# A decoder block's attention on one core: output projections in whole groups of four, spread over the last two batches, and one token tile of the last batch projected before the next stage

## The chip, the cores and the metric

The kernel runs on one core of one Trainium2 chip. The metric is the device time of a run in microseconds (us). The kernel before took 2040.6 us as the median of three runs (2039.63 to 2043.01). The profile is one further execution with the hardware profiler on.

## The reference

One pre-norm decoder block on x of 4 batches x 512 tokens x 512 features, all in fp32.

```python
x = x + attn(layernorm(x), weight_qkv, weight_proj)      # causal, 16 query heads, 4 key/value groups, D = 128
x = x + xattn(layernorm(x), ctx, ctx)                    # 32 query heads, 8 key/value heads, D = 16
x = x + ffn(layernorm(x), gate_w, w1, w2, w3, sw1, sw2, sw3)  # 8 experts, top 2, plus a shared expert

def attn(x, weight_qkv, weight_proj):
    qkv = einsum('bsh,ph->bsp', x, weight_qkv)           # per group: 4 query heads, a key, a value
    scores = where(causal, q @ k.T / sqrt(128), lowest)
    out = softmax(scores) @ v                            # 2048 features per token
    return einsum('bse,he->bsh', out, weight_proj)
```

Only the first line's attention and its neighbour, the cross-attention, are touched by the change.

## The kernel before

The program has three stages: causal attention (to about 889 us of the span), cross-attention with the shared expert as filler (to about 1600 us), and the routed experts.

**The attention stage** goes through 64 slots, one for each unit (b, g, h): batch, key/value group, query head of the group. I number them 0 to 63 in that order, so batch b has slots 16b to 16b + 15, and slot 4g + 3 of a batch ends a group. TensorE's instructions keep the program's order (`pinned_mm`, `Ordered`, L128 to 147), so the loop at L398 writes PE's order out by hand. The other engines' order is set by a scheduler, unless `pinned` is on. A slot does two things at once:

- `scores(u)` (L322) for its own unit: four score blocks of 128, 256, 384 and 512 columns (PE, tile `sc`); a causal mask and a negated maximum for each (DVE, `nmx`); an exp with its sum (ACT, `pr`); at the end the division by the sum (DVE).
- `attend(held)` (L359) for the unit before: the weights are transposed in four parts of 1, 2, 3 and 4 blocks (PE, `tp`), copied out of PSUM (`prT`: DVE, the second part ACT), multiplied with the values (`po`), and copied by ACT into `oT`.

Between these steps the loop drops single matmuls, called jobs, from two lists. `ahead` holds what the next slot needs: its query projection (`project`, L289: four jobs, tile `pq`, evicted by ACT into `qT`) and, ahead of a new group, the key projection as well (four more, `kT`). `waiting` holds what may come later: value projections (`values`, L267, tile `pv`) and, once a group of four heads is done, its output projections (`output`, L308): for each of four token tiles a product of four jobs (tile `pj`), which DVE then adds to x. A slot takes as many waiting jobs as `take` says: 8, 8, 0, 0 in the first group, then 4, 5, 5, 2 over a group's four slots. `room` tells how many jobs follow each of the eight steps; `ahead` is served first.

Every such product fills one PSUM tile with tag "mm", of which there are two (`product`, L253; the pool at L187 gives two to each of the tags `t`, `mm`, `sc`, `po`). So a product that is half done keeps one of the two until its last job. In a batch's last slot the next batch's normalised x is turned (`turn`, L243: four transposes, tile `xt`, copied by ACT into `xnT`), and the first projections of that batch follow at once. After a batch's first slot its sixteen value projections come in one piece. `norm_first` (L226) normalises batch 0 tile by tile: statistics and the scaling on DVE, the power -0.5 on GpSimd (POOL); it isn't pinned.

The last batch's output projections are left to the next stage. There, `fill` (L870) gets four products of sixteen jobs each (tile `pl`, one for each token tile, over all 16 heads), in one PSUM bank with tag "fill".

**The cross-attention stage** (L900) runs 32 units of 8 steps, numbered i. Step i computes two heads' scores row-wise for their maxima (`row_maxima`, PE `s`, DVE `cnmx`) and, 11 steps later (`LAG`), the same scores turned for the exponentials (`weights`, PE `s`, ACT `w`). Each of the two has three PSUM banks. Every second step, `gather` multiplies the weights with the values (`cpo`). Jobs of `fill` go first, around the transposes `tc` and `tx` (8 + 5 + 4 jobs, L894 to 899); then one per step for 11 steps; then, up to step 80 (`SWAP`), the rest is spread over every second step (L924):

```python
elif i < SWAP:
    if mstep % 2 == 0:
        run(fill, -(-2 * len(fill) // (SWAP - i)))
```

Of the kernel before, what the change touches and what calls it, by code (L numbers as in the profile page):

```python
# [8 lines left out]
F32 = mybir.dt.float32  # L9
BF16 = mybir.dt.bfloat16  # L10
AF = mybir.ActivationFunctionType
ALU = mybir.AluOpType
# [3 lines left out]
P = 128  # L16
B, S, HID = 4, 512, 512
NT = S // P
NC = HID // P
NKV, QPG, D = 4, 4, 128  # L20
# [10 lines left out]
EPS = 1e-5  # L31
# [4 lines left out]
def decoder_kernel(  # L36
# [15 lines left out]
    nc = tc.nc  # L52
# [80 lines left out]
    pinned_mm, pinned = True, False  # L133

    class Ordered:
# [12 lines left out]
    tensor, vector, scalar, gpsimd, sync = (  # L148
        Ordered(e) for e in (nc.tensor, nc.vector, nc.scalar, nc.gpsimd, nc.sync)
    )  # L150

    xb = [xpool.tile([P, NT, HID], F32, tag=f"x{b}", name=f"x{b}") for b in range(B)]
# [31 lines left out]
    with ExitStack() as ph:  # L184
        wp = ph.enter_context(tc.tile_pool(name="wattn", bufs=1))
        p2 = ph.enter_context(tc.tile_pool(name="a2", bufs=2))
# [6 lines left out]
        wqk, wpr = [], []  # L193
        for g in range(NKV):
            t = wp.tile([P, NC, (QPG + 1) * D], F32, tag=f"wqk{g}", name=f"wqk{g}")
# [5 lines left out]
            t = pj.tile([P, QPG, HID], F32, tag=f"wpr{g}", name=f"wpr{g}")  # L201
# [12 lines left out]
        xns, xnTs, vs, kTs, qTs, outs = {}, {}, {}, {}, {}, {}  # L214
# [10 lines left out]

        def norm_first():  # L226

            xns[0] = []
            for s in range(NT):
                xn = p2.tile([P, HID], F32, tag="xn", name=f"xn0_{s}", bufs=4)  # L230
                st = small.tile([P, 6], F32, tag="st", name=f"fst{s}")
                mv = small.tile([P, 2], F32, tag="fmv", name=f"fmv{s}")
                nc.vector.bn_stats(st, xb[0][:, s, :])
                nc.vector.bn_aggr(mv, st)
                rstd = small.tile([P, 1], F32, tag="frstd", name=f"frstd{s}")
                nc.vector.tensor_scalar(rstd, mv[:, 1:2], EPS, None, ALU.add)
                nc.gpsimd.tensor_tensor(rstd, rstd, mhalf[:, 0:1], ALU.pow)
                nc.vector.tensor_scalar(
                    xn, xb[0][:, s, :], mv[:, 0:1], rstd, ALU.subtract, ALU.mult
                )  # L240
                xns[0].append(xn)

        def turn(b, s):  # L243

# [8 lines left out]
        def product(name, operands, done):  # L253
            held = []

            def job(k, lhsT, rhs):
                if k == 0:
                    held.append(ps.tile([P, S], F32, tag="mm", name=name))
                tensor.matmul(
                    held[0], lhsT=lhsT, rhs=rhs, start=k == 0, stop=k == len(operands) - 1  # L260
                )
                if k == len(operands) - 1:
                    done(held[0])

            return [lambda k=k, o=o: job(k, *o) for k, o in enumerate(operands)]

        def values(b):  # L267
            jobs, vs[b] = [], {}
# [53 lines left out]
        def scores(u):  # L322

            b, g, h = u
            qT, kT = qTs.pop(u), kTs[b, g]
            pr = p2.tile([P, 10 * P], F32, tag="pr", name=f"pr{b}_{g}_{h}")
            nmx = small.tile([P, NT], F32, tag="nmx", name=f"nmx{b}_{g}_{h}")
            sm = small.tile([P, NT], F32, tag="sm", name=f"sm{b}_{g}_{h}")

            def part(i):  # L330
                n = (i + 1) * P
                sc = ps.tile([P, S], F32, tag="sc", name=f"sc{b}_{g}_{h}_{i}")
                tensor.matmul(
                    sc[:, :n], lhsT=qT[:, i * P : n], rhs=kT[:, :n], start=True, stop=True
                )
                nc.vector.tensor_tensor(  # L336
                    sc[:, i * P : n], sc[:, i * P : n], maskf, ALU.add
                )
                nc.vector.tensor_reduce(  # L339
                    nmx[:, i : i + 1], sc[:, :n], AX.X, ALU.max, negate=True  # L340
                )
                nc.scalar.activation(  # L342
                    pr[:, OFF[i] : OFF[i] + n],
                    sc[:, :n],
                    AF.Exp,
                    bias=nmx[:, i : i + 1],
                    accum_out=sm[:, i : i + 1],
                )

            def divide():  # L350
                rs = small.tile([P, NT], F32, tag="rs", name=f"rs{b}_{g}_{h}")
                nc.vector.reciprocal(rs, sm)
                for j in range(NT):
                    w = pr[:, OFF[j] : OFF[j] + (j + 1) * P]
                    nc.vector.tensor_scalar(w, w, rs[:, j : j + 1], None, ALU.mult)

            return pr, [lambda i=i: part(i) for i in range(NT)], divide
# [31 lines left out]


        units = [(b, g, h) for b in range(B) for g in range(NKV) for h in range(QPG)]
        norm_first()
        for s in range(NT):
            turn(0, s)
        for job in project(0, 0, QPG) + project(0, 0, 0):
            job()
        waiting, ahead, held = values(0), [], None
        for u in units + [None]:  # L398
            between, turns = [lambda: None] * NT, []
            take = 4  # L400
            if u is not None:
                b, g, h = u
                pr, between, divide = scores(u)
                if (b, g) == (0, 0):
                    take = 8 if h < 2 else 0
                else:
                    take = (4, 5, 5, 2)[h]
                if (g, h) == (NKV - 1, 1) and b + 1 < B:
                    norm(b + 1)
                if h + 1 < QPG:  # L410
                    ahead = project(b, g, h + 1)
                elif g + 1 < NKV:
                    ahead = project(b, g + 1, QPG) + project(b, g + 1, 0)
                elif b + 1 < B:
                    turns = [lambda s=s: turn(b + 1, s) for s in range(NT)]

            room = [1, 1, 1, 1, 1, 1, 0, 2] if held else [1, 1, 1, 1, 0, 0, 0, 0]
            total = min(take, len(waiting)) + len(ahead) + (8 if turns else 0)
            for k in (1, 2, 0, 3, 7, 5, 4) * 2:
                room[k] += sum(room) < total  # L420
            for k in (5, 4, 0, 3, 2, 1) * 2:
                room[k] -= sum(room) > total and room[k] > 0
            steps = attend(*held) if held else []
            for k in range(2 * NT):
                if k < NT:
                    between[k]()
                    if turns:
                        turns.pop(0)()
                        if not turns:
                            ahead = project(b + 1, 0, QPG) + project(b + 1, 0, 0)  # L430
                elif steps:
                    steps.pop(0)()
                for _ in range(room[k]):
                    some = ahead or waiting
                    if some:
                        some.pop(0)()
            for job in ahead:
                job()
            ahead = []
            for step in steps:  # L440
                step()
            if u is not None:
                divide()
            if held:
                b_, g_, h_ = held[0]
                if h_ == QPG - 1 and b_ < B - 1:
                    waiting += output(b_, g_)
                if h_ == QPG - 1 and g_ == NKV - 1 and b_ < B - 1:
                    for job in values(b_ + 1):
                        job()  # L450
            held = (u, pr) if u is not None else None
        assert not waiting
        last_outs = [outs[B - 1, g] for g in range(NKV)]


# [114 lines left out]
    with ExitStack() as ph:  # L570
        p1 = ph.enter_context(tc.tile_pool(name="c1", bufs=1))
        p2 = ph.enter_context(tc.tile_pool(name="c2", bufs=2))
# [29 lines left out]
        for b in range(B):  # L602
            t = p1.tile([P, NT, XKV * XD], F32, tag=f"ctx{b}", name=f"ctx{b}")
# [264 lines left out]
            return ps.tile([P, S], F32, tag=tag, name=name, bufs=3 if tag == "s2" else 1)  # L868

        jobs, fill, po, last, oT = [], [], None, None, None  # L870
        for s in range(NT):
            group(
                fill,
                bank,
                f"pl{s}",
                [
                    (last_outs[g][h][:, s * P : (s + 1) * P], wpr[g][:, h, :])
                    for g in range(NKV)
                    for h in range(QPG)
                ],  # L880
                add_to(B - 1, s),
            )
# [8 lines left out]
        moments, turn = enter(0)  # L891
        run(moments, len(moments))
        pinned = True
# [6 lines left out]
        for i in range(NU * 8 + LAG + 4):  # L900
            n, step = divmod(i, 8)
# [34 lines left out]
            b, u = divmod(n, XKV)  # L936
            if b < B - 1:
                if u == XKV - 3 and step == 0:
                    moments, turn = enter(b + 1)
# [12 lines left out]
            if oT is not None and mstep == 3:  # L952
                add_heads(*oT)
                if oT[0] % XKV == XKV - 1 and oT[0] < NU - 1:
                    b = oT[0] // XKV
                    parts, tokens = route(b)
# [15 lines left out]
        parts, tokens = route(B - 1)  # L972
# [3 lines left out]
        parts = logits(B - 1, single, lambda lg: chosen.extend(choose(B - 1, lg)))  # L976
# [343 lines left out]
```

## Time and profile before

| what | value |
|---|---|
| median of three runs | 2040.6 us |
| the profiled execution | 2043.63 us |
| its span, first to last instruction | 2041.7 us |
| mean granted TensorE clock | 0.996 |
| first matmul | 8.89 us |
| first score of slot 0 | 20.78 us |
| first `pl` job | 889.42 us |
| first score of the cross-attention | 907.53 us |
| last `pl` job | 1082.96 us |

In the rows that follow, PE is TensorE's matmuls, PEld its weight loads, DVE VectorE, ACT ScalarE, POOL GpSimd and SP the queue that issues most DMAs. Almost all matmuls have line 141, that of the helper which keeps their order, so they are told apart by tile names, out<-in. An fp32 matmul has two records, a transpose one. A row of the timeline has its start, the time that it covers, engine, line, operation, tiles, shapes, the number of instructions merged into it, and, in brackets, idle time ahead of it with the engine that ended it. A row of the waits has who waited for whom, the total in us, how often, and the longest.

### The profile page before, as it was taken

Reading aid. Unit: us, or ns where it says so; the run is one execution under the profiler, and the core shown is the slowest. Engines: PE = TensorE matmul, PEld = TensorE weight load, DVE = VectorE, ACT = ScalarE, POOL = GpSimd, SP = SyncE. Lnnn points to the kernel's source line nnn. Section 1 sums busy time; section 2 is a strip of 40 time slices with the busy share of each in tenths; the row PEclk is TensorE's granted clock in tenths of the full one; section 3 lists DMA queues with packets and bytes.
Section 4 is the critical chain, followed back from the end, with each engine's and each line's share of the span. In section 5 each row is a group of like instructions: output and inputs, shape, how many; then the busy total and the mean of one; then the engine's idle time right before and its main releaser. Section 6 shows DMA issues by size and latency. Waiting matters only on the chain. (4 is left out here: it accounts for less than half of the span.)

```text
span 2041.7 us, 22321 instructions
## 1 busy us (share of the span) xinstructions
PE 1996.7 (98%) x8251; PEld 934.3 (46%) x8251; DVE 936.0 (46%) x2100; ACT 681.0 (33%) x1479; POOL 199.0 (10%) x185
## 2 busy tenths in 40 slices
PE   7999999999999999999999999999999999999997
PEld 4555555554555555542233333333333345655564
DVE  5544355453444345546666656565664251111111
ACT  2322232332232323423555454444444201222221
POOL 1000000000000000010202201120200000333331
PEclk9999999999999999999999999999999999999999
DMA  8000000000000000010003100100010075333331
GB/s 288 0 0 1 1 0 1 0 0 0 1 0 1 0 0 0 1 33 14 15 17 87 48 12 22 48 12 17 17 48 7 31 258 154 63 61 62 64 57 22
DMA packets 52555, 74.77 MB, mean 37 GB/s; under 512 B 9937, under 2 KB 27857, under 8 KB 52450
## 3 DMA queue, kind: packets, MB, share of 16 engines
q1 hardware_dynamic: 43714, 54.73, 8.8%
q0 software_dynamic: 8736, 18.62, 5.1%
q8 instruction: 67, 1.10, 0.2%
q14 instruction: 38, 0.31, 0.1%
HBM read 47.60 MB, written 18.61 MB: 32 GB/s over the span
## 5 line engine op out<-in xcount | busy, mean ns | idle before, releaser
L141 DVE TENSOR_REDUCE cnmx<-s 128x1 f32<-128x512 f32 x512 | 329.5, 685 | 199.7 <-PE s L141 199.6
L141 ACT ACTIVATE w<-s 128x512 f32<-128x512 f32 x512 | 277.9, 594 | 339.2 <-PE s L141 339.1
L141 PE MATMUL pq<-xnT,wqk 128*128 128x512 f32 x640 | 317.1, 595 | 10.8 <-ACT kT L295 8.1
L141 PE MATMUL s<-ckT,cqT 32*128 32x512 f32 x1024 | 308.7, 640 | 1.0 <-DVE cnmx L141 1.0
L141 PE MATMUL s<-cqT,ckT 32*128 32x512 f32 x1024 | 294.7, 640 | 0.0
L336 DVE TENSOR_TENSOR sc<-sc,maskf 128x128 f32<-128x128 f32 x256 | 76.6, 299 | 371.6 <-PE sc L141 371.5
L141 PE MATMUL pj<-wpr,oT 128*128 128x512 f32 x384 | 187.3, 593 | 0.0
L342 ACT ACTIVATE pr<-sc,nmx 128x128 f32<-128x128 f32 (+3 forms) x256 | 135.0, 527 | 153.3 <-DVE nmx L339 153.2
L141 PE MATMUL sc<-kT,qT 128*128 128x128 f32 (+3 forms) x512 | 179.3, 437 | 1.5 <-ACT pr L342 0.8
L141 PE MATMUL sh<-fnT,sw 128*128 128x512 f32 x320 | 154.0, 612 | 0.0
L141 PEld LDWEIGHTS pq<-xnT,wqk 128*128 128x128 f32 x640 | 112.9, 190 | 87.5 <-issue 47.4
L141 PE MATMUL po<-prT,v 128*128 128x512 f32 (+3 forms) x512 | 148.6, 433 | 1.6 <-DVE prT L371 1.6
L141 PEld LDWEIGHTS s<-cqT,ckT 32*128 32x128 f32 x1024 | 80.8, 183 | 145.8 <-ACT w L141 108.1
L141 PE MATMUL cpo<-w,vpad 128*32 128x512 f32 x1024 | 137.2, 608 | 0.0
L141 PEld LDWEIGHTS po<-prT,v 128*128 128x128 f32 x512 | 96.2, 190 | 83.5 <-issue 47.1
L141 PEld LDWEIGHTS sc<-kT,qT 128*128 128x128 f32 x512 | 89.2, 190 | 92.9 <-issue 78.7
L339 DVE TENSOR_REDUCE nmx<-sc 128x1 f32<-128x128 f32 (+3 forms) x256 | 125.6, 490 | 8.3
L384 ACT COPY oT<-po 128x512 f32<-128x512 f32 x64 | 37.5, 586 | 244.3 <-PE po L141 244.3
L141 PEld LDWEIGHTS tp<-ident,pr 128*128 128x128 f32 x640 | 78.3, 141 | 79.6 <-issue 36.6
L141 PE MATMUL y<-w3all,hT 128*128 (+1 forms) x234 | 107.3, 594 | 3.1 <-ACT yo L1232 2.5
L141 PE MATMUL tp<-ident,pr 128*128 128x128 f32 x640 | 100.5, 274 | 4.3 <-DVE prT L371 3.5
L141 PE MATMUL h<-w1all,xT 128*128 x312 | 98.7, 459 | 0.9 <-issue 0.9
(164 smaller groups left out, 1932.1 us busy)
## 6 DMA issues: line engine op xcount, KB each, us to landing
w1all<-in_w1T SPq DMA_DIRECT2D x8, 704.0 KB
w2all<-in_w2T SPq DMA_DIRECT2D x8, 704.0 KB
wqk<-in_wqkvT SPq DMA_DIRECT2D x4, 1280.0 KB
wpr<-in_wprojT SPq DMA_DIRECT2D x4, 1024.0 KB
cqT<-cxnT SPq DMA_DIRECT2D x128, 32.0 KB
ckT<-ctxT SPq DMA_DIRECT2D x128, 32.0 KB
normed<-fxn SPq DMA_DIRECT2D x4, 1024.0 KB
out<-x SPq DMA_DIRECT2D x16, 256.0 KB
```

Of the source, the lines that this page charges most:

```text
L141: i = getattr(self.engine, name)(*args, **kw)
L336: nc.vector.tensor_tensor(sc[:, i * P : n], sc[:, i * P : n], maskf, ALU.add)
L339: nc.vector.tensor_reduce(nmx[:, i : i + 1], sc[:, :n], AX.X, ALU.max, negate=True)
L342: nc.scalar.activation(pr[:, OFF[i] : OFF[i] + n], sc[:, :n], AF.Exp, bias=nmx[:, i : i + 1], accum_out=sm[:, i : i + 1],)
L384: nc.scalar.copy(o, po)
```

## The change

Five things are changed in the attention stage, and one follows in the next.

- `norm_first` is written as a pipeline (statistics of a tile ahead of the scaling of the tile before), and DVE keeps that order, since `pinned` is on.
- Two value jobs are run ahead of slot 0; the first group takes 6, 8, 0, 0.
- All other slots take 4; in the last two batches a group's slots take 4, 2, 2, 4.
- In a batch's last slot, after the last turn, waiting jobs come ahead of the next batch's projections (`late`).
- The first token tile of the last batch (16 jobs, tile `pl0`) joins `waiting` at slot 60; slots 60 to 63 take 3 each, and the final pass, which has no unit of its own, takes what is left but one, which comes last of all.
- So `fill` has 48 jobs instead of 64.

```diff
-            xns[0] = []
-            for s in range(NT):
-                xn = p2.tile([P, HID], F32, tag="xn", name=f"xn0_{s}", bufs=4)
+            xns[0], parts = [], []
+
+            def moments(s):
                 st = small.tile([P, 6], F32, tag="st", name=f"fst{s}")
                 mv = small.tile([P, 2], F32, tag="fmv", name=f"fmv{s}")
-                nc.vector.bn_stats(st, xb[0][:, s, :])
-                nc.vector.bn_aggr(mv, st)
                 rstd = small.tile([P, 1], F32, tag="frstd", name=f"frstd{s}")
-                nc.vector.tensor_scalar(rstd, mv[:, 1:2], EPS, None, ALU.add)
+                vector.bn_stats(st, xb[0][:, s, :])
+                vector.bn_aggr(mv, st)
+                vector.tensor_scalar(rstd, mv[:, 1:2], EPS, None, ALU.add)
                 nc.gpsimd.tensor_tensor(rstd, rstd, mhalf[:, 0:1], ALU.pow)
-                nc.vector.tensor_scalar(
+                parts.append((mv, rstd))
+
+            def apply(s):
+                mv, rstd = parts[s]
+                xn = p2.tile([P, HID], F32, tag="xn", name=f"xn0_{s}", bufs=4)
+                vector.tensor_scalar(
                     xn, xb[0][:, s, :], mv[:, 0:1], rstd, ALU.subtract, ALU.mult
                 )
                 xns[0].append(xn)
+
+            moments(0)
+            for s in range(1, NT):
+                moments(s)
+                apply(s - 1)
+            apply(NT - 1)
...
-            return [lambda k=k, o=o: job(k, *o) for k, o in enumerate(operands)]
+            return [
+                lambda k=k, o=o: job(k, *(o() if callable(o) else o))
+                for k, o in enumerate(operands)
+            ]
...
+        pinned = True
         norm_first()
+        pinned = False
...
         waiting, ahead, held = values(0), [], None
-        for u in units + [None]:
+        for _ in range(2):
+            waiting.pop(0)()
+        for n, u in enumerate(units + [None]):
             between, turns = [lambda: None] * NT, []
-            take = 4
+            take = 4 if u is not None else len(waiting) - 1
             if u is not None:
                 b, g, h = u
                 pr, between, divide = scores(u)
                 if (b, g) == (0, 0):
-                    take = 8 if h < 2 else 0
-                else:
-                    take = (4, 5, 5, 2)[h]
+                    take = (6, 8, 0, 0)[h]
+                elif b >= B - 2:
+                    take = (4, 2, 2, 4)[h]
+                if n == len(units) - 4:
+                    waiting += product(
+                        "pl0",
+                        [
+                            lambda g=g, h=h: (outs[B - 1, g][h][:, 0:P], wpr[g][:, h, :])
+                            for g in range(NKV)
+                            for h in range(QPG)
+                        ],
+                        lambda t: nc.vector.tensor_tensor(
+                            xb[B - 1][:, 0, :], t, xb[B - 1][:, 0, :], ALU.add
+                        ),
+                    )
+                if n >= len(units) - 4:
+                    take = 3
...
                 for _ in range(room[k]):
-                    some = ahead or waiting
+
+                    late = k == NT - 1 and g == NKV - 1 and h == QPG - 1 and ahead
+                    some = waiting if late and waiting else ahead or waiting
                     if some:
                         some.pop(0)()
...
-        assert not waiting
+        for job in waiting:
+            job()
...
-        for s in range(NT):
+        for s in range(1, NT):
             group(
                 fill,
                 bank,
                 f"pl{s}",
```

## The prediction

> **What bounds the kernel now.** I read the page first (engine shares, then the costliest groups), then the longest waits of PE in the attention stage, then the timeline of single slots, and last the timeline of two pairs of steps of the cross-attention. The page:
>
> ```profile
> PE 1996.7 (98%) x8251; PEld 934.3 (46%) x8251; DVE 936.0 (46%) x2100; ACT 681.0 (33%) x1479; POOL 199.0 (10%) x185
> ...
> L141 PE MATMUL pq<-xnT,wqk 128*128 128x512 f32 x640 | 317.1, 595 | 10.8 <-ACT kT L295 8.1
> ...
> L141 PE MATMUL pj<-wpr,oT 128*128 128x512 f32 x384 | 187.3, 593 | 0.0
> ```
>
> PE is busy for 98% of the span, so a change of order can only win back its idle moments, or shorten steps in which PE counts as busy but waits inside. After the bar stands the idle time before a group: query and key projections (pq) lose 10.8 us, 8.1 of it to the key's eviction, while output projections (pj) lose nothing. The waits of PE between 20 and 890 us, longest in total first, say how often:
>
> ```profile
> PE pq L141 <- ACT kT L295: 8.1, 12, 0.7
> PE tp L141 <- DVE prT L371: 3.5, 15, 0.3
> PE pq L141 <- ACT xnT L250: 2.0, 3, 0.7
> PE po L141 <- DVE prT L371: 1.6, 2, 0.8
> PE tp L141 <- ACT prT L371: 0.9, 3, 0.3
> ```
>
> Ends of matmuls are modelled, so I count in starts: a record of 512 columns takes 0.43 us from start to start, a projection (two records) 0.859. In starts, the 12 kT waits lose 0.95 each (projection at 753.39 instead of 752.55, plus 0.10 after it), the three xnT waits the same. The timeline of one slot with four output projections (762.76 to 775.04) shows the chain through which a transposing slot runs:
>
> ```profile
> 767.50 1.02 PE L141 MATMUL pq<-xnT,wqk 128*128 128x512 f32 x2
> 768.35 0.27 PE L141 MATMUL tp<-ident,pr 128*128 128x128 f32 x1
> 768.46 1.02 PE L141 MATMUL pj<-wpr,oT 128*128 128x512 f32 x2
> 768.55 0.60 ACT L299 ACTIVATE qT<-pq 128x512 f32<-128x512 f32 x1 [0.98 <-PE pq L141]
> 769.05 0.68 ACT L342 ACTIVATE pr<-sc,nmx 128x512 f32<-128x512 f32 x1
> 769.80 0.37 ACT L371 COPY prT<-tp 128x256 f32<-128x256 f32 x1
> 770.40 0.93 PE L141 MATMUL tp<-ident,pr 128*128 128x128 f32 x7
> ```
>
> The last four transposes need the bank that ACT's prT copy frees, and that copy stands behind qT and the last exp on ACT. Here it costs nothing, because two output projections lie between the transposes. In the cross-attention, the same engine's rows show a pair of steps with one pl projection in it (982.59) and one without (from 1097.20):
>
> ```profile
> 981.26 0.69 PE L141 MATMUL s<-cqT,ckT 32*128 32x512 f32 x1
> ...
> 982.59 1.12 PE L141 MATMUL pl<-wpr,oT 128*128 128x512 f32 x2
> ...
> 985.71 0.69 PE L141 MATMUL s<-cqT,ckT 32*128 32x512 f32 x1
> ...
> 989.90 0.69 PE L141 MATMUL s<-cqT,ckT 32*128 32x512 f32 x1
> ...
> 1097.20 0.69 PE L141 MATMUL s<-cqT,ckT 32*128 32x512 f32 x1
> ...
> 1099.15 0.69 PE L141 MATMUL s<-ckT,cqT 32*128 32x512 f32 x1
> ...
> 1101.19 0.69 PE L141 MATMUL s<-cqT,ckT 32*128 32x512 f32 x1
> ```
>
> With a pl a pair takes 989.90 - 985.71 = 4.19 us, without one 3.99: the second step's scores come piecemeal (1098.16 to 1099.68), each behind an exp or a maximum. A pl there costs 0.20, not 0.86.
>
> [...]
>
> **The change, part by part.** All instructions stay, in another order; 16 pl projections (13.7 us of PE) move from the cross-attention into the attention stage. SP's and POOL's queues issue the same work in the same order, except that the POOL selection for `before` is put between the small powers of the first norm; no DMA moves. I take slots 0 to 63 (b, g, h in order) from the built order and price each kind by starts.
>
> Kinds shown before: four pq and four pj, 12.28 (762.76 to 775.04); five pj, 13.14 (721.54 to 734.68); eight pq and two pj with the kT wait, 14.94 (747.82 to 762.76); four pq alone, 9.50 (775.04 to 784.55), of which 0.67 is holes, so 8.83 of work; a batch's last slot, 20.21 (676.81 to 697.02), with two holes of 0.95; a batch's first slot, 24.52 (697.02 to 721.54), with 1.09 of holes.
>
> New kinds. B, eight pq and a whole group: 14.94 - 0.95 + 2 x 0.859 = 15.71; both banks are free, and the two pq between each pair of scores hide the kT copy. T, last slot: eight pj instead of five, two of them while xnT is copied (0.67 of idle), so 20.21 - 1.90 + 3 x 0.859 = 20.89. C, half a group, both projections after the transposes: nothing now lies between the transposes. Put at T the first transpose (768.35): qT, exp and prT copy end at 769.73 + 0.36, four transposes restart 0.06 later, 1.80 after T instead of 0.66. Hole 1.14. The nearest row is the slot at 697.02, whose restart came at 703.44, 1.50 after its first transpose, with qT not ahead of the exp; 0.30 for qT makes 1.80 again. Bounds: 0.67, all the holes of a slot with nothing in it, and 1.22, if the copy starts at 769.80 as here. C = 8.83 + 1.72 + 1.14 = 11.69.
>
> Sums. Slots 5 to 14 were six of 13.14, two of 12.28, two of 14.94 (133.3); now eight of 12.28 and two B (129.7): -3.6. Slots 17 to 30: eight, three and three of those kinds (186.8) become eleven of 12.28 and three B (182.2): -4.6. Slots 33 to 46: the same 186.8 becomes eight C, three of 12.28, three B (177.5): -9.3. T three times: +2.0. Slots 16 and 32 lose a pj and part of the holes: 13.74 (sixteen pv) + 9.50 - 24.52 = -1.28 each, -2.6. Slot 48 gains three pj and loses its holes: +1.5. Slots 49 to 58 were 113.3; six C, two of 12.28 and two B make 126.1: +12.8, for twelve more pj (10.3) and 2.5 more of holes. Slots 60 to 62, three pl in each, one of them between transposes, leaving a hole of 0.30: 8.83 + 2.58 + 0.30 = 11.71 for 9.50, +6.6. Slot 63 and the end (875.61 to the first fill at 889.42): seven pl, 6.0, of which 2.8 cover the waits at 877.21, 881.51 and 886.32; but the last pl must wait for the last oT, as the first fill does now, and then pl1 waits for its eviction, as at 906.47 (1.0 in starts): +4.0. Together +6.8.
>
> The start: the norm in program order lets the first transposes run about 1 us earlier, and two pv cover the 0.85 before 20.78. But batch 1's x lands at 19.73, and DVE now puts three of batch 1's four xn writes ahead of the first score's mask, one before: the mask moves from 24.36 by two writes (0.46 each), the third score with it to 26.8 from 25.85. With one more pv done by then (0.86), the gain is gone: 0, between -1.9 (all of it stays) and +0.5.
>
> The cross-attention: `fill` has 48 jobs, not 64. Its first 28 go the same way. Steps 11 and 13 then take one job instead of two: -1.9 (two of about 0.95). From step 15 on it is one per pair: before to step 77, now to step 49, so 14 pairs fall from 4.19 to 3.99: -2.8. Bounds for such a pair: 3.1, what is left of PE's work (two times 1.06 of scores and 1.0 of cpo), and 4.36, twice the mean step of the twelve without fill from 1084.69 to 1114.45 (first maximum of each), after their transposes are taken off (29.8 - 3.6 over 12 is 2.18).
>
> Waits added: the pl1 wait above; and on DVE the eviction of pl0 stands behind four cxn writes (1.92 us from 888.94). They start after the last po, 1.6 before that pl ends, so they are just done; up to 1.9 if they wait for the last pl instead. I take 0.
>
> Sum: +6.8 + 0 - 1.9 - 2.8 = +2.1. The profiled execution took 2043.63 us (span 2041.7); that becomes a span of 2043.8. It lies 3.0 above the median of the runs (2040.6), so I carry the difference over: 2042.7.
>
> **The rivals.** A measurement tells 0.2%, 4.1 us, from no change. Forecast: within that, 2042.7; its own range, the start, C and pairs varying inside their bounds, 2036.5 to 2044.7. Slower: steps without fill give nothing back. They ran at 2.18 in the stretch from 1084.69, against 2.10 with fill; bn_stats and fnT copies lay beside them there, which speaks against it. At 4.36 a pair the cross-attention loses 2.4 instead of winning 2.8: +7.3, 2047.9. It decides from 4.13 a pair with the sum above (4.1 - 4.9 = -0.8, over 14 pairs -0.06 from 4.19), from 4.0 if the cxn wait comes too. Faster by the cross-attention: pairs at PE's 3.1 give -15.3, -10.4 in all, 2030.2; DVE has 2.6 of maxima in a pair and would allow it, but three banks and the measured 3.99 speak against it. Faster by the transposes: C at 0.67 (ACT not in the way) gives 14 x 0.47 = 6.6, so -4.5, 2036.1; the order on ACT speaks against it. That the change doesn't do what it says: the kT waits stay, because a half group is still open at the key; +8.6, but no slot of the built order has one open there.
>
> **How the numbers follow.** Forecast 0.53; slower 0.29, with C at its upper bound and the cxn wait leading there too; faster 0.18 (0.08 by the pairs, 0.10 by C together with the start). The range leaves out the pairs at PE's pace and reaches to the slower case: 2035 to 2048.
>
> **What would show it.** Right: no wait of pq for kT or xnT; 14 waits of tp for ACT's prT copy, each with about 1.1 us in starts; the first fill some 7 us later; pairs of about 4.0 between steps 51 and 77. Wrong: tp waits under 0.7 us, pairs near 3.1 or over 4.2, a first score before 20.0 that keeps its lead past slot 1, or an extra wait ahead of the first fill.

## The result

The change made the kernel slower: 2048.35 us (median of 14 runs, 2044.28 to 2051.44) against 2043.01 us for the kernel before on the same chip (14 runs, 2038.11 to 2046.81). The ratio is 1.0028, 95% interval 1.0018 to 1.0038, so 3.7 to 7.8 us. The forecast was +2.1 us, within 0.2%. (It stood on a base of 2040.6 us, the median of three runs; fourteen runs put the base 2.4 us higher, so the ratio is the fair comparison.) The profiled execution of the changed kernel took 2051.37 us, with a span of 2049.5 (before: 2043.63 and 2041.7).

The page of the changed kernel, its engine shares and the groups that the prediction was about (after the last bar: idle time ahead of the group and what ended most of it):

```profile
PE 2008.2 (98%) x8251; PEld 945.4 (46%) x8251; DVE 944.8 (46%) x2100; ACT 678.1 (33%) x1479; POOL 200.0 (10%) x185
...
L141 PE MATMUL pq<-xnT,wqk 128*128 128x512 f32 x640 | 317.6, 597 | 0.7 <-ACT xnT L261 0.7
...
L141 PE MATMUL pj<-wpr,oT 128*128 128x512 f32 x384 | 186.5, 593 | 0.0
...
L141 PE MATMUL po<-prT,v 128*128 128x512 f32 (+3 forms) x512 | 150.1, 436 | 2.5 <-DVE prT L385 2.5
...
L141 PE MATMUL tp<-ident,pr 128*128 128x128 f32 x640 | 102.4, 276 | 12.4 <-ACT prT L385 8.6
```

The projections lost nearly all of their 10.8 us of idle time, as intended. The transposes' idle time rose to 12.4 us, in the direction of the forecast; in the kernel before their row was

```profile
L141 PE MATMUL tp<-ident,pr 128*128 128x128 f32 x640 | 100.5, 274 | 4.3 <-DVE prT L371 3.5
```

The row of `po` grew from 1.6 us, two waits of at most 0.8, to 2.5. The waits of PE between 20 and 905 us (who waits for whom, total, times, longest) show that it is now a single wait:

```profile
PE tp L141 <- ACT prT L385: 8.6, 17, 0.6
PE tp L141 <- DVE prT L385: 3.8, 20, 0.3
PE po L141 <- DVE prT L385: 2.5, 1, 2.5
PE pl L141 <- DVE x L436: 1.0, 1, 1.0
```

No wait for kT or xnT is left. The waits of `tp` for ACT's copy are those of the fourteen slots C, with half a group, and of slots 60 to 62. A slot C in the changed kernel shows the order on ACT that the prediction had described:

```profile
486.78 0.60 ACT L313 ACTIVATE qT<-pq 128x512 f32<-128x512 f32 x1 [0.98 <-PE pq L141]
...
487.27 0.68 ACT L356 ACTIVATE pr<-sc,nmx 128x512 f32<-128x512 f32 x1
...
487.94 0.37 ACT L385 COPY prT<-tp 128x256 f32<-128x256 f32 x1
...
488.36 0.66 PE L141 MATMUL tp<-ident,pr 128*128 128x128 f32 x4 [0.58 <-ACT prT L385]
```

The copy follows the exp, and the exp follows qT, with no idle time between them. The one wait of 2.5 us lies in slot 62. Its timeline in the changed kernel, all engines in order of time:

```profile
872.99 1.02 PE L141 MATMUL pq<-xnT,wqk 128*128 128x512 f32 x2
...
874.08 0.98 POOL L141 MEMSET rows<- 4x512 f32 x2 [565.95 <-PE pq L141]
...
875.01 1.92 POOL L141 MEMSET cqT<- 128x512 f32 x4
875.56 4.20 DVE L369 TENSOR_SCALAR pr<-pr,rs 128x128 f32<-128x128 f32 x1
...
876.87 1.91 POOL L141 MEMSET ckT<- 128x512 f32 x4
...
878.74 2.35 POOL L141 MEMSET vpad<- 128x1024 f32 x3
879.82 0.67 DVE L385 COPY prT<-tp 128x512 f32<-128x512 f32 x1
...
880.55 3.98 PE L141 MATMUL po<-prT,v 128*128 128x512 f32 x8 [2.45 <-DVE prT L385]
```

POOL had waited for the last `pq` of the attention stage; after it, POOL clears tiles of the next stage (`rows`, `cqT`, `ckT`, `vpad`), which take over memory of this one. Right in those MEMSETs DVE starts slot 62's division by the sum. Its first product, 128x128, takes 4.20 us (875.56 to 879.77); it ends just after the first of `vpad`'s MEMSETs, at 879.68. The prT copy behind it on DVE ends at 880.49, and PE stands from 878.1 to 880.55. Then `po` itself takes 3.98 us instead of the 2.32 of other slots. The same place in the kernel before:

```profile
871.74 1.88 PE L141 MATMUL pq<-xnT,wqk 128*128 128x512 f32 x4
...
872.78 1.27 DVE L355 TENSOR_SCALAR pr<-pr,rs 128x128 f32<-128x128 f32 x4
...
873.68 1.28 POOL L141 MEMSET rows<- 4x512 f32 x2 [560.72 <-PE pq L141]
...
881.58 1.27 DVE L355 TENSOR_SCALAR pr<-pr,rs 128x128 f32<-128x128 f32 x4
```

There the last `pq` lay behind the transposes, so the MEMSETs came when slot 62's division was nearly over, and slot 63's came after the long series: four products in 1.27 us each time. The `pl` jobs had pushed the last `pq` ahead of the transposes, and so the MEMSETs on to the division. Slot 62 took 16.11 us (868.26 to 884.37); slots 60 and 61 took 11.83.

By place, changed kernel minus kernel before, in starts: up to slot 60 -2.5 (forecast -3.8), slots 60 to 62 +11.3 (forecast +6.6), slot 63 to the next stage's first fill +4.2 (forecast +4.0), from there to the shared expert's first matmul -5.0 (forecast -4.7): +7.9, which is the difference of the two spans (7.8). The first fill came 12.9 us later, where the prediction had said some 7. The medians differ by 5.3: the profiled execution of the changed kernel lies 3.0 above the median of its runs, that of the kernel before 0.6 above the median of the fourteen.

In all eleven profiles the stretch from the shared expert's first matmul to the routed experts takes 515.5 to 518.9 us though nothing was edited there. The granted TensorE clock accounts for it: the traces' record of that clock has stretches of 3.41 us, or of twice that, in which half of the clock was granted. Five profiles have none of them in that part (515.5 to 515.7 us), two have 3.41 us of them (517.2), and four have 6.83 us (518.8 to 518.9). So 3.41 us at half clock cost about 1.7 us, and how many of them fall into an execution varies. The whole times go with it: of the 43 runs of the kernel before that were taken with the first four experiments, those with a mean granted clock of 0.998 or 0.999 took 2038.25 to 2040.80 us, those with 0.996 2042.56 to 2046.61. So below, places are compared by their own starts, and whole kernels by their ratios.

### The profile page after: what moved, and what is told of

It is laid out like the page before. It is cut to its first block, busy times and chain, and to the rows that moved or that the text cites. A ratio compares the mean times of both kernels' runs of the same rounds, so it can differ in the third digit from the quotient of the medians.

```text
span 2049.5 us, 22311 instructions
## 1 busy us (share of the span) xinstructions
PE 2008.2 (98%) x8251; PEld 945.4 (46%) x8251; DVE 944.8 (46%) x2100; ACT 678.1 (33%) x1479; POOL 200.0 (10%) x185
## 5 line engine op out<-in xcount | busy, mean ns | idle before, releaser
L141 PE MATMUL s<-ckT,cqT 32*128 32x512 f32 x1024 | 319.9, 642 | 1.0 <-DVE cnmx L141 1.0
L141 PE MATMUL s<-cqT,ckT 32*128 32x512 f32 x1024 | 304.2, 641 | 0.0
L141 PEld LDWEIGHTS s<-cqT,ckT 32*128 32x128 f32 x1024 | 85.7, 184 | 145.4 <-ACT w L141 107.7
L141 PE MATMUL tp<-ident,pr 128*128 128x128 f32 x640 | 102.4, 276 | 12.4 <-ACT prT L385 8.6
L385 DVE COPY prT<-tp 128x128 f32<-128x128 f32 (+2 forms) x192 | 97.4, 527 | 28.3 <-PE tp L141 27.8
```

The costliest lines, as they stand in the source:

```text
L141: i = getattr(self.engine, name)(*args, **kw)
L385: copy(prT[:, : i + 1, i * P : (i + 1) * P], t[:, : i + 1, :])
```

## The experiments

Each ratio is to the kernel before on the same chip, with its 95% interval; the changed kernel stands at 1.0028.

**Slot 62 with its last projections behind the transposes.** The changed kernel with:

```diff
             steps = attend(*held) if held else []
+            if n == len(units) - 2:
+                ahead = [waiting.pop(0) for _ in range(take)] + ahead
```

so that the three `pl` go first.

> The changed kernel, but in slot 62 the three pl jobs come first and the four pq last, two of them behind the transposes. Theory: in the changed kernel GpSimd's MEMSETs, released by the last pq, ran at 874.1 to 881.9 over slot 62's division and held VectorE's 128x128 TENSOR_SCALAR for 4.20 us, so that po came 2.6 us late in starts. With the last pq after the transposes the MEMSETs start some 3 us later, when the division is done: it takes about 0.3 us again, the wait of po for prT (2.45 us) goes, slot 62 takes 11.6 to 11.9 us instead of 16.11 (1.65 of which was the throttle), and the time is 2.6 us under the changed kernel's, 1.0015 of the kernel before. Rival: the division is late for another reason (the deeper slot 62), and the wait of about 2.5 us stays where it is; 1.0028 of the kernel before.

Measured: 2044.16 us, ratio 1.0004 (0.9995 to 1.0012). Its timeline:

```profile
875.18 0.55 DVE L369 TENSOR_SCALAR pr<-pr,rs 128x128 f32<-128x128 f32 x2
...
876.11 1.88 PE L141 MATMUL pq<-xnT,wqk 128*128 128x512 f32 x4
...
877.83 2.32 PE L141 MATMUL po<-prT,v 128*128 128x512 f32 x8
...
878.06 0.98 POOL L141 MEMSET rows<- 4x512 f32 x2 [570.04 <-PE pq L141]
```

The MEMSETs come 4 us later, two products take 0.55 us, `po` doesn't wait, and slot 62 takes 11.83 us, 4.28 less. That is more than the 2.6 us that I had expected: the slow `po` went too.

**The same order, but another instruction for the division.** The first experiment also moved projections. This one moves nothing; only slot 62's four products change their kind, to see whether the MEMSETs hold all that DVE does or only this instruction:

```diff
+                    if u == units[-2]:
+                        many = rs[:, j : j + 1].to_broadcast([P, (j + 1) * P])
+                        nc.vector.tensor_tensor(w, w, many, ALU.mult)
+                        continue
                     nc.vector.tensor_scalar(w, w, rs[:, j : j + 1], None, ALU.mult)
```

> The changed kernel with its order unchanged, but slot 62's division is written as a TENSOR_TENSOR with the reciprocal broadcast along the row, in place of a TENSOR_SCALAR. Theory: [...] Then the MEMSETs still run at 874 to 882, the four products take 0.2 to 0.6 us each beside them, and po waits under 0.2 us for prT instead of 2.45: 2.6 us under the changed kernel, 1.0015 of the kernel before. Rival: VectorE is held by the MEMSETs whatever it does in SBUF: a first product of about 4 us, and po still waits 2.4 us; 1.0028.

Measured: 2044.22 us, ratio 1.0006 (0.9998 to 1.0015).

```profile
875.11 1.92 POOL L141 MEMSET cqT<- 128x512 f32 x4
875.66 0.29 DVE L371 TENSOR_TENSOR pr<-pr,rs 128x128 f32<-128x128 f32 x1
875.87 0.55 DVE L389 COPY prT<-tp 128x384 f32<-128x384 f32 x1
...
876.34 0.41 DVE L371 TENSOR_TENSOR pr<-pr,rs 128x256 f32<-128x256 f32 x1
...
876.98 1.92 POOL L141 MEMSET ckT<- 128x512 f32 x4
...
878.03 2.32 PE L141 MATMUL po<-prT,v 128*128 128x512 f32 x8
```

With the same MEMSETs beside it, the product takes 0.29 us instead of 4.20, and slot 62 again 11.83. So it isn't the depth of the slot: the MEMSETs hold up the TENSOR_SCALAR (4.20 us), and not a TENSOR_TENSOR (0.29) or a copy out of PSUM (0.55 for the 128x384 one above). What ties the two engines in this way is not shown. The product of the changed kernel, started at 875.56, sat through the rest of `cqT`'s MEMSETs, all of `ckT`'s and the first of `vpad`'s. Why it got through there, with more MEMSETs to come, is open.

**What made `po` slow after the pause.** The stretches of the changed kernel around it (per stretch: length, busy time of PE, PEld, DVE, ACT, POOL with counts, then PEclk, the granted TensorE clock, DMA share, GB/s):

```profile
878.00:880.00 2.00, 0.10 (x1) 0.00 (x0) 2.00 (x4) 0.00 (x0) 2.00 (x4) 1.00 0.24 70
880.31:883.72 3.41, 3.17 (x5) 1.53 (x6) 1.49 (x3) 0.00 (x0) 1.57 (x4) 0.50 0.37 87
884.00:886.00 2.00, 2.00 (x11) 1.18 (x9) 1.14 (x4) 1.04 (x3) 0.00 (x0) 1.00 0.00 0
```

PE is idle in the first, and from 880.31 to 883.72 half of the clock is granted: `po` takes about 1.65 us more, on top of the pause. In the kernel with the other division the clock is at 1.00 from 878 to 886. The half clock came with the pause in all three further kernels below that have one (0.50 granted from 883 to 885 us in the last batch's token tile alone, from 876 to 877 in the half groups, from 861.2 to 866.2 in the better order), and the seven profiles without the pause have no entry of half clock in the attention stage; so I count it to the price of the pause, 4.28 us in all. (Without such a pause it came later, as at 1090.38 in the kernel before; see the result.) In the changed kernel and the first two of these three, PE had waited 2.5 us for prT ahead of it, in the better order 5.0 us for the exp; how long a pause it takes is not shown.

**The last batch's token tile alone.** The kernel before with the `pl0` part of the diff and nothing else (`take = 3` from slot 60 on, the product put into `waiting`, `fill` from tile 1 on).

> The kernel before, but with the last batch's first token tile projected in slots 60 to 63 and the final pass as in the changed kernel, and nothing else changed. Theory: slots 60 and 61 take 11.83 instead of 9.50 (+4.7), slot 62 takes 16.1 instead of 9.50 (+6.6, 4.3 of it the division held by the MEMSETs and the half clock after the pause), slot 63 and the end +4.2, and the cross-attention gives back 5.0: +10.5 us, 1.0051 of the kernel before. The prediction's numbers for the same part were +6.6 + 4.0 - 4.7 = +5.9, 1.0029. Rival: the stall in slot 62 needs the rest of the change (its pj in the slots ahead) and doesn't appear here: +6.2, 1.0030.

Measured: 2051.98 us, ratio 1.0040 (1.0026 to 1.0053). Slots 60 to 62 take 11.83, 11.83 and 16.20, and the shared expert's first matmul comes 10.05 us later than before. The waits name the stall once more, next to the kT waits that this kernel keeps:

```profile
PE pq L141 <- ACT kT L298: 8.1, 12, 0.7
...
PE po L141 <- DVE prT L374: 2.5, 1, 2.5
```

So the stall needs nothing of the rest. Both the expected 1.0051 and the rival's 1.0030 lie in the interval; the slots decide, not the ratio.

**The change without that part.** The changed kernel with the `pl0` lines removed, `take = 4` in the final pass and 64 jobs in `fill`.

> The changed kernel, but the last batch's first token tile goes back to the cross-attention: 64 jobs in fill, none in slots 60 to 63. Theory: the 16 jobs cost 13 us of TensorE in the attention stage and gave back only 5.0 in the cross-attention. Back in fill: slots 60 to 62 fall to 9.50 each (-7.0), the 2.6 of slot 62 and its wait of po go, slot 63 with the tail falls by 4.2, the cross-attention grows by 5.0: 8.8 us under the changed kernel, 0.9985 of the kernel before. Rival: the slots' jobs are nearly free there and it is the C slots that made the change slow: within 2 us of the changed kernel, 1.002 to 1.003.

Measured: 2037.37 us, ratio 0.9968 (0.9957 to 0.9979). Up to the shared expert it is 10.7 us ahead of the changed kernel; the expectation had left the half clock out. From the first transpose of the context to the shared expert it takes 231.4 us with 64 jobs in `fill`, the changed kernel 226.6 with 48: sixteen jobs, 13.7 us of TensorE elsewhere, cost 4.8 there. In slots 60 to 63 and the final pass the same sixteen cost 15.4 us (slots 60 to 62 11.3, the rest 4.2), and 11.2 without the stall. So without its `pl0` part the change would have been a gain, and the stall is only part of the loss: moving the tile cost some 6 us more than it gave back even where nothing was held up, as the prediction's own terms (+6.6 + 4.0 - 4.7) had it.

**Half groups with a projection between the transposes.** The changed kernel with:

```diff
+            if held and total in (4, 6):
+                room = [0, 1, 1, 0, 1, 0, 0, 1] if total == 4 else [1, 1, 1, 1, 1, 0, 0, 1]
+                ahead = [waiting.pop(0) for _ in range(total - 4)] + ahead
             steps = attend(*held) if held else []
```

> The changed kernel, but in the 14 slots with half a group (C) the two pj come first, and of the four pq one lies between the transposes and one behind them. Theory: C's hole of 1.19 us (0.33 + 0.74) is ACT doing qT and the exp ahead of the prT copy that the last four transposes wait for; with one projection between the transposes and qT only after them the hole falls to 0.1 or less, C from 11.74 to about 10.65, in all 14 x 1.09 = 15.3 us: 0.7450 % under the changed kernel, 0.9953 of the kernel before. Rival: the hole comes from VectorE or from the exp itself and stays at 0.67, as in slots with four pq alone: 14 x 0.52 = 7.3 us, 0.9992. No gain at all would mean that the hole moves to the next slot's scores, behind the late qT.

Measured: 2040.58 us, ratio 0.9988 (0.9981 to 0.9995), by the ratios 8.2 us under the changed kernel. C takes 11.16 instead of 11.74 in thirteen slots and 11.44 in one: 7.8 us. (The edit also reorders slots 2, 4, 16 and 32, which have four `pq` alone; they take 0.13 longer each.) That is close to the rival's 7.3 and far from the expected 15.3, and the timeline of one C slot tells why:

```profile
487.57 1.02 PE L141 MATMUL pq<-xnT,wqk 128*128 128x512 f32 x2
...
487.87 0.69 ACT L356 ACTIVATE pr<-sc,nmx 128x512 f32<-128x512 f32 x1 [1.18 <-DVE nmx L353]
488.43 0.71 PE L141 MATMUL tp<-ident,pr 128*128 128x128 f32 x5
...
488.91 0.37 ACT L385 COPY prT<-tp 128x256 f32<-128x256 f32 x1 [0.26 <-PE tp L141]
489.33 0.66 PE L141 MATMUL tp<-ident,pr 128*128 128x128 f32 x4 [0.19 <-ACT prT L385]
```

ACT is now idle ahead of the copy: neither qT nor the exp is in its way. What is left is the way itself, transposes to copy to transposes, because the projection stands behind the first part, whose copy DVE makes, and not behind the second, whose copy ACT makes (0.35 us). The remaining 0.19 lies ahead of and in `po`, since one projection doesn't quite cover the last prT copy. Slots 60 and 61 of the changed kernel, with one job in that same place but qT ahead of the exp, have the same 0.35. So this run can't tell qT's share from the job's, and the rival's reason, that the hole comes from VectorE or from the exp, isn't shown by it either.

**The start alone.** The kernel before with the new `norm_first`, the two early value jobs and 6, 8, 0, 0.

> The kernel before with the start of the changed kernel alone: norm_first as a pipeline in program order, two value jobs ahead of slot 0, 6, 8, 0, 0 in the first group. Theory: nothing is won, since the first transposes come 2.7 us earlier but the granted clock reaches full speed later (16.7 us instead of 11.8 in the changed kernel), so slot 1 starts at 33.8 us instead of 33.46: +0.3, within 0.1 % of the kernel before. Rival (the prediction's lower bound): the earlier transposes carry through, slot 1 starts near 31.6, -1.9 us, 0.9991.

Measured: 2041.93 us, ratio 0.9993 (0.9985 to 1.0002); slot 1 starts at 33.77, as expected. The sixteen records of the first two projections, in this kernel:

```profile
11.73 9.74 PE L141 MATMUL pq<-xnT,wqk 128*128 128x512 f32 x16 [0.68 <-ACT xnT L261]
```

and in the kernel before:

```profile
12.96 7.13 PE L141 MATMUL pq<-xnT,wqk 128*128 128x512 f32 x16 [0.68 <-ACT xnT L250]
```

They begin 1.2 us earlier and take 2.6 us longer: the first six are 0.85 to 1.01 us apart instead of 0.43. That is half pace, after transposes that now come in short bursts, each waiting for its own xn. The granted clock goes with it. The trace's record of the clock begins, at full speed, at 17.02 us in this kernel, and the spacing falls to 0.43 at 17.01; in the kernel before it begins at 11.77, ahead of the first projection. (For the time before its first entry the column of the granted clock reads 1.00, which says nothing.) In all six kernels with the new start the record begins between 15.6 and 17.5 us, in the five with the old one between 10.9 and 12.9. That the pauses between the transposes are what delays it is not shown. In the kernels that kept the old order, slot 1 started anywhere from 32.69 to 34.20, so no effect of the start can be claimed beyond that it wins nothing visible.

**Whole groups alone.** The kernel before with one line:

```diff
-                    take = (4, 5, 5, 2)[h]
+                    take = 4
```

> The kernel before with take = 4 in place of 4, 5, 5, 2 from the second group on, and nothing else changed (the last slots of a batch still open half a group ahead of the next batch's projections). Theory: the nine waits of pq for kT inside the batches go (9 x 0.95 in starts), the three at the batches' last slots and the three for xnT stay, the number of slots with nothing but pq stays seven: -8.6 us, 0.9958 of the kernel before. Rival: in slots with eight pq and a whole group the wait moves to another bank or to ACT, and a slot takes more than 15.72: half of it or less, 0.998 or more.

Measured: 2033.91 us, ratio 0.9954 (0.9942 to 0.9967). All twelve kT waits are gone, also those of the last slots; the waits now begin with

```profile
PE tp L141 <- DVE prT L371: 3.4, 15, 0.3
PE pq L141 <- ACT xnT L250: 2.0, 3, 0.7
```

Slots with eight `pq` and a whole group take 15.71, as the prediction had put B. By starts, this one line brings the first fill of the next stage 10.5 us forward, against 2.6 for the whole change without `pl0` (whose ratio, 0.9968, overlaps in its interval): that one had also spread the groups, and paid 14 holes of 1.19 us for it, about half of which it saved in other slots.

**A better order.** From the kernel before: `take = 4`; `late` as in the changed kernel; the last four `pj` kept for slot 63; and in slots with four `pq` alone

```diff
+            if held and u is not None and total == len(ahead) == 4:
+                room = [0, 1, 1, 0, 0, 1, 0, 1]
```

> The kernel before with whole groups in every slot, waiting jobs ahead of the next batch's projections in a batch's last slot, all 64 pl jobs left in the cross-attention, the start as before; in slots with four pq alone one pq lies behind the second part of the transposes and one behind them all; and the last group of pj is kept for slot 63. Theory, by starts: 12 kT and 3 xnT waits gone (-14.2), slots 16, 32 and 48 lose about 0.7 each of their holes (-2.1), slots with four pq alone fall from 9.50 to about 9.2 (-2.0), the four pj cover about 1.8 in slot 63: -20 us, 0.9902 of the kernel before, first fill near 869.5. Rival: the pq behind the second part leaves the hole that it left behind the first part (0.35 + 0.19), so bare slots stay at 9.6 and slots 16, 32, 48 at 23.4: -15 us, 0.9927.

Measured: 2026.87 us, ratio 0.9918 (0.9906 to 0.9931), not the 0.9902. The projection behind the second part does fill the hole of the transposes (bare slots 9.25). But slot 63 took 18.10 us:

```profile
852.40 7.77 DVE L355 TENSOR_SCALAR pr<-pr,rs 128x128 f32<-128x128 f32 x4
...
852.45 0.98 POOL L141 MEMSET rows<- 4x512 f32 x2 [544.65 <-PE pq L141]
...
860.09 0.28 DVE L336 TENSOR_TENSOR sc<-sc,maskf 128x128 f32<-128x128 f32 x1
```

One projection fewer behind the transposes, and the MEMSETs met the division again: my own order fell into the trap that I had just measured. The first product was held although it had started 0.05 us ahead of the first MEMSET, and again it ended (858.14) just after the first of `vpad`'s MEMSETs (858.06). PE waited 5.0 us for slot 63's exp and then ran at half clock, until 866.22. Hence the last kernel, with slots 62 and 63 divided by TENSOR_TENSOR:

> The kernel of e8_best with the division of slots 62 and 63 written as a TENSOR_TENSOR with the reciprocal broadcast. In e8_best the last pq came one projection ahead of slot 62's end, so the MEMSETs (852.5 to 860.3) met slot 62's division at 852.40: its four TENSOR_SCALARs took 7.77 us, slot 63's first mask stood behind them, PE paused for 5.0 us and then ran at half clock for some 2.5 us. Theory: written as TENSOR_TENSOR the division isn't held, slot 63 takes about 10.6 us instead of 18.10, the half clock goes with the pause: -7.5 us, 0.9881 of the kernel before. Rival: the MEMSETs also hold a TENSOR_TENSOR when they started first or when it is long (512 columns), so that 3 us or more of the pause stay: 0.990 or more.

Measured: 2022.57 us, ratio 0.9900 (0.9881 to 0.9919).

```profile
851.29 1.70 DVE L357 TENSOR_TENSOR pr<-pr,rs 128x128 f32<-128x128 f32 x4
...
851.34 0.98 POOL L141 MEMSET rows<- 4x512 f32 x2 [544.65 <-PE pq L141]
...
853.91 0.30 DVE L336 TENSOR_TENSOR sc<-sc,maskf 128x128 f32<-128x128 f32 x1 [0.92 <-PE sc L141]
```

Slot 63 takes 10.61 us, as expected, and the first fill comes at 868.64, 20.8 us earlier than in the kernel before. This is the fastest version, about 21 us under the kernel before and 26 under the changed one. The ratio, a little short of 0.9881, also touches the rival's 0.990; here too the slot decides. Between the context's first transpose and the routed experts this profile is 4.9 us longer than that of the run above, with the same program there: it has half clock there for 3.41 us from 1069.66 and for 6.83 us from 1615.80, the run above none. At the price found with the result, about 1.7 us for each 3.41, that is the difference.

## Why the prediction was wrong

- **Waits for kT and xnT, and B, T:** right. No such wait after 20 us is left; B took 15.72 against 15.71 in the prediction, T 20.90 against 20.89.
- **C:** right in mechanism, as the rows of ACT with the result show, and nearly in size: 11.74 against 11.69, hole 1.19 against 1.14, 14 times, +0.7 in all.
- **Slots 60 to 62:** the step that failed. "Slots 60 to 62, three pl in each ... 11.71 for 9.50, +6.6" priced each slot by what PE itself waits for: two of the three came out at 11.83, and slot 62 at 16.11. Behind it stands the sentence "SP's and POOL's queues issue the same work in the same order", which I took for no cost. The order was the same, the moment wasn't: the MEMSETs hang on the last `pq`, the `pl` jobs move that `pq` ahead of the transposes, and DVE's division is held up. The slots grew by 11.3 us instead of 6.6, and 4.28 of that is the stall with the half clock after it. Of the prediction's signs of being wrong, the extra wait ahead of the first fill is the one that came. Two experiments that take the stall away, one by the order and one by the kind of instruction, bring slot 62 to 11.83 and the whole kernel to 1.0004 and 1.0006, in the forecast's reach of "within 0.2%".
- **Slot 63 and the end:** right, +4.2 against +4.0, with the wait of `pl1` for its bank.
- **The start:** right at about 0 (slot 1 starts 0.3 us later), not for the reason given, so by luck. The early lead was lost in the first projections at half pace, ahead of the point where I had lost it to batch 1's xn writes.
- **The cross-attention:** right. -5.0 against -4.7. In the changed kernel the maxima's scores of an unfilled pair start here:

```profile
1051.91 0.69 PE L141 MATMUL s<-cqT,ckT 32*128 32x512 f32 x1
...
1055.91 0.69 PE L141 MATMUL s<-cqT,ckT 32*128 32x512 f32 x1
```

  4.00 us, against 3.99 in the prediction. The rivals' 3.1 and 4.36 didn't come in such pairs.
- **The slower rival** ended near the measured time (2047.9) by another way: its mechanism, steps without fill that give nothing back, is refuted by these 4.00 us. None of the rivals had the stall in it.

By place the sum came out 5.8 us over the forecast (+7.9 against +2.1). Of this, 4.28 are the one missing term, which was enough to turn "same" into "slower"; the rest is small, most of it in C, the start and slots 60 to 62.

## What to carry to other kernels

A queue whose order doesn't change can still move in time: for every instruction that is moved, ask who waits for its end, also in the next stage (memory that is handed on), and what that work will run beside. Filler is worth what it costs where it lies: here sixteen projections cost about 5 us in steps that wait anyway, and 11.2 in slots that PE already fills, or 15.4 with the stall. When single executions differ, look at the granted clock before looking for a cause in the kernel. Order products so that none is half done when another kind needs the bank; here that one line, `take = 4`, was worth 0.46%.

## What the runs showed of the hardware

- Beside GpSimd MEMSETs that followed each other without a pause, VectorE's SBUF-to-SBUF TENSOR_SCALAR was held through many of them: a 128x128 product took 4.20 us in the changed kernel and, with its three fellows, 7.77 us in the better order (1.27 for the four in the kernel before). In both it got through at the end of the first 128x1024 MEMSET (879.77 against 879.68, 858.14 against 858.06). A TENSOR_TENSOR of the same shape took 0.29 us beside them, a 128x384 copy from PSUM 0.55.
- With a pause of PE of 2.45 us, half of the clock was granted for 3.41 us (880.31 to 883.72), and all of it from 878 to 886 in the kernel with the other division, which has no pause: `po` took 3.98 us against 2.32, about 1.65 more.
- Half clock also came in stretches of 3.41 or 6.83 us elsewhere, in some executions and not in others, at about 1.7 us for each 3.41. In these kernels that accounts for the 515.5 to 518.9 us of one unedited stretch.
- At the start, transposes in short bursts were followed by six projection records 0.85 to 1.01 us apart, until the clock's record began at 17.02 us (the start alone); after transposes in one piece (the kernel before) the first was 0.53 and the others 0.43 us apart, with a record from 11.77 us.
